# Where the attention's residual is turned for the ffn: from PE transposes to GpSimd's reordering, reads between the ffn's bursts and 32x32 turns on DVE

## The chip, the cores and the metric

The kernel runs on one core of one Trainium2 chip. The time is the device time of one execution in microseconds (us). The kernel before took 1957.53, 1955.65 and 1949.80 us in three runs; the median, 1955.65, is the time that the change is measured against.

In the profile's lines PE is TensorE's matmul unit, PEld its weight loading, DVE VectorE, ACT ScalarE, POOL GpSimd, SP SyncE (which here only issues DMAs); a q behind an engine's name is its queue of DMA issues. L1211 is line 1211 of the kernel before.

## What is computed

Two images of 128 channels and 64 x 64 positions pass two layers; everything is float32. Layer 0 (group norm, neighbourhood attention over 7 x 7 positions, layer norms and linear maps) isn't touched by the change. Layer 1 treats the 4096 positions as tokens `t` of 128 channels:

```python
t = _to_tokens(x)                       # [2, 4096, 128]
t = t + _L1_attn_ref(_ln_t(t))          # full self-attention, diagonal masked
t = t + _L1_ffn_ref(_ln_t(t), ...)
return _from_tokens(t, x)               # [2, 128, 64, 64]

def _stu(u, sigma, phi, Mu, Mpp, Mpm):  # what the ffn computes, for each of 4 lengths
    return _compute_spectral(u, sigma, phi, Mpp, Mpm) + _compute_ar_u(Mu, u)

def _compute_ar_u(Mu, u):               # three lags, each with a 128 x 128 matrix
    for i in range(Mu.shape[0]):
        ui = jnp.pad(u, ((0, 0), (i, 0), (0, 0)))[:, :sl]
        out = out + jnp.einsum('btd,de->bte', ui, Mu[i])
```

`_compute_spectral` convolves u causally with 16 filters along the tokens, once with and once without alternating signs, and applies a 128 x 128 matrix for each filter. The four lengths (all tokens, a half, a quarter, an eighth) are weighed by a hard choice (gumbel softmax). The change concerns the second line, `t + attention`, which has to be there twice: normalised as the ffn's input, and as it is, as the residual that the ffn's output is added to.

## The kernel before

**Stages.** Layer 0 takes the first 346 us. Then come the attention of image 0 (to about 720 us), that of image 1 (to about 1137), a tail that finishes image 1's last tokens (to 1199.6), the ffn of both images (to about 1920) and the last outputs.

**The attention** works on chunks of 512 tokens, eight to an image. Exponentials are made once for a pair of chunks (tiles `e`, 128 x 2048), sent through DRAM (`eb`) in 32-row pieces and turned by DVE, 32 x 32 at a time, into `et`, for the pair's other half. The chunk's result, channels by tokens, gathers in `xa[b]`. Work that isn't attention is handed out in small steps: after each step of the attention `fill()` takes the next step of the generators that wait, the urgent ones first.

**after(b, c)** is such a generator, one for each chunk that is complete. Four PE transposes bring xa's chunk to tokens by channels; DVE divides by the softmax's sum and adds it onto `tt[b]`, tokens by channels, so that `kept_` is the chunk of `t + attention`. Then come its layer norm (with a power on GpSimd), the transpose of the normalised tokens into `zc[b]`, channels by tokens, and the ffn's first transform: products with `tr` into two PSUM banks, which `store` copies into `uo` (ACT), adds and subtracts into `ub` (GpSimd; in the tail one of the two on DVE) and sends to `us` in DRAM. A chunk has four such stores of 128 rows (256 KB each), and its last 32 rows go out as eight small ones. During attention `fresh` queues these stores on GpSimd's queue, where `fill` issues them; in the tail (`crowd_[0] is None`) SP issues them at once. `ub` has four buffers and `uo` two.

**short_lags(b, h)** runs once for each half of an image. It first brings the residual into channels by tokens: four times, four PE transposes of `tt[b]` into a bank and a copy by ACT into `xa[b]` (L1209 to L1211). Then it makes four products of three lags each (L1221) out of `zc[b]`, and four DVE operations (six, where a length's boundary cuts the chunk) scale each by the branch's weight and add it onto xa (L1237). `residual_of` takes the first four steps in attention and the products are kept for later (`kept`, `held`); image 1's second half has its lags in the tail and the first bursts of the ffn.

**The tail** (L1547 on): the remaining chunks' generators take turns, and image 1's first lags are handed out between them; then the second half's transposes and two of its products.

**The ffn** has 160 blocks, 80 of each image. `burst` makes one block's 16 matmuls (K = 32 rows each, four at a time), four copies from PSUM into `y` (DVE, ACT, DVE, ACT) and starts the loads of a block four ahead: `ct` in four DMAs and `ut` in one, all on SP. `ct` has five buffers, `ut` four. Four bursts make one `y` (a group). `project` multiplies y by the filters' matrices, 16 k's for each of two signs, in the banks acc0 to acc3; a burst of the next group stands before every eighth k. `mixed_bins` empties the banks with four copies into `af` (DVE, ACT, DVE, ACT) and makes ten additions on GpSimd. `back` does the inverse transform of an image's first sixteen groups and adds it onto xa; `finished` does that of its last four and sends the output. Everything that is added onto xa must be there before `finished(b)` reads it. Only PE's order is written out by hand (`manual_schedule`); that of the other engines is made by the scheduler. The tiles of the ffn lie in the memory that the tail's tiles leave.

Of the kernel before, what the change touches and what calls it, by code (L numbers as in the profile page):

```python
# [14 lines left out]
P = 128  # L15
# [87 lines left out]
def kernel(  # L103
# [771 lines left out]
    gs = dram.tile([Q, 2, 2, SG, GROW], F32, name="gs")  # L875

    with ap_:
# [211 lines left out]
        queued_, turns_, crowd_ = [], [0, 0], [[]]  # L1089
# [28 lines left out]
        def after(b, c):  # L1118
# [19 lines left out]
            nc.vector.tensor_tensor(kept_[:, :, P - 1], kept_[:, :, P - 1], rest, ALU.subtract)  # L1138
            yield
# [14 lines left out]
            def store(pu, n, r0, m, ri):  # L1154

                for s in range(2):
                    both = sp.tile([P, 512], F32, tag="uo", name="uo", bufs=2)
                    nc.scalar.copy(both[:, 0 : 2 * n], pu[s][:, 0 : 2 * n])  # L1158
                    room()
                    ub = sp.tile([P, 2, 256], F32, tag="ub", name="ub", bufs=4)  # L1160
                    for sgn, op in enumerate((ALU.add, ALU.subtract)):
                        adder[sgn].tensor_tensor(ub[:, sgn, 0:n], both[:, 0:n], both[:, n : 2 * n], op)  # L1162
                    to = us[b, par, r0 : r0 + m, :, :, 2 * hh + s, 2 * fp : 2 * fp + 2]
                    if ri is not None:
                        fresh(to[:, :, ri].rearrange("k g f d -> k g (f d)"), ub)
                        continue
                    for sgn in range(2):
                        for f in range(2):
                            fresh(to[:, sgn, :, f].rearrange("k i d -> i k d"), ub[64 * f : 64 * f + 64, sgn, 0:P])
# [33 lines left out]
        def short_lags(b, h):  # L1203


            for par in range(2):
                n0 = (par * 2 + h) * 8
                for f0 in range(0, 8, 4):
                    pt = bank()  # L1209
                    transposed(pt, tt[b][:, n0 + f0 : n0 + f0 + 4, :])  # L1210
                    nc.scalar.copy(xa[b][:, (n0 + f0) * P : (n0 + f0 + 4) * P], pt)  # L1211
                    yield
            for par in range(2):
                for part_ in range(2):
# [16 lines left out]
                    for lo, hi in cut:  # L1231
                        t0 = c0 + lo * BLK
                        s = 0 if t0 < 256 else 1 if t0 < 512 else 2 if t0 < 1024 else 3
                        for e in range(2):
                            for i in range(NFP):
                                xs = xv[:, e, i, :, p0 + lo : p0 + hi]
                                nc.vector.scalar_tensor_tensor(  # L1237
                                    xs, pv[:, e, i, :, lo:hi], seg[:, s : s + 1], xs, ALU.mult, ALU.add
                                )
# [162 lines left out]
        def residual_of(lags):  # L1402
            for _ in range(4):
                next(lags)
                yield

        def filler(b, steps, kept, slow=()):
# [5 lines left out]
            def fill(c=None):  # L1413
                if c is not None:
                    done.append(c)
                    urgent.append(after(b, c))
                    if len(done) % 4 == 0:
                        lags = short_lags(b, len(done) // 4 - 1)
                        if kept is not None:
                            kept.append(lags)  # L1420
                            lags = residual_of(lags)
                        urgent.append(lags)
# [125 lines left out]
        *chains, residuals = left  # L1548
# [8 lines left out]
        for _ in residuals:  # L1557
            next(kept[0], None)
            next(held, None)
# [3 lines left out]
        for _ in range(2):  # L1563
            next(lags)
# [7 lines left out]
    with ExitStack() as cv:  # L1572
# [158 lines left out]

        order_ = [(b, q) for b in range(NB) for q in range(K2)]
# [3 lines left out]
        with tc.manual_schedule(engines={mybir.EngineType.PE}):  # L1736
            y = new_y()
            for i in range(4):
                if i % 2 == 0:
                    next(lags, None)  # L1740
# [10 lines left out]
            for i, (b, g) in enumerate(groups):  # L1751
# [3 lines left out]
                for l in range(2):  # L1755
                    for k in range(KF):
                        if following is not None and k % 8 == 0:
                            burst(following, 2 * l + k // 8)
                        project(y, acc, l, k)
# [138 lines left out]
```

## Time and profile before

| | us |
|---|---|
| median of the three runs | 1955.65 |
| the profiled execution | 1954.66 |
| its span, from first to last instruction | 1952.80 |

The span in stages, from the busy times of the engines in windows (us):

| stage | from, to | length | PE | DVE | ACT | POOL | DMA share |
|---|---|---|---|---|---|---|---|
| layer 0 | 0, 346 | 346.0 | 315.3 | 283.2 | 261.9 | 221.5 | 0.25 |
| attention, image 0 | 346, 720 | 374.0 | 370.4 | 189.0 | 116.9 | 152.7 | 0.67 |
| attention, image 1 | 720, 1137 | 417.0 | 412.6 | 189.2 | 126.6 | 180.0 | 0.68 |
| tail | 1137, 1199.6 | 62.6 | 55.7 | 37.1 | 18.1 | 17.8 | 0.25 |
| ffn | 1199.6, 1920 | 720.4 | 715.7 | 250.4 | 202.1 | 161.5 | 0.25 |
| last outputs | 1920, 1952.8 | 32.8 | 21.4 | 7.1 | 5.7 | 4.2 | 0.16 |

A row reads: in the ffn's 720.4 us PE was busy 715.7. The DMA share is that of the core's 16 DMA engines. Four groups of instructions by line, on which the change bears:

```profile
L1211 ACT COPY xa<-bank 128x512 f32<-128x512 f32 x16 | 9.1, 592 | 15.8 <-PE bank L202 15.8
L974 DVE STREAM_TRANSPOSE et<-et 128x512 f32<-128x512 f32 x216 | 134.2, 678 | 70.9 <-DMA et<-eb 70.8
L598 POOL COPY rb<-rden 128x512 f32<-128x512 f32 x16 | 9.8, 611 | 4.5 <-DVE rden L593 4.5
L1237 DVE SCALAR_TENSOR_TENSOR xa<-bank,seg,xa 128x128 f32<-128x128 f32 (+1 forms) x72 | 17.9, 312 | 7.0 <-PE bank L1221 7.0
```

The columns are: the line, the engine and operation, the tile written and those read, their shapes, and how many; then the busy time of all in us and the mean of one in ns; then the engine's idle time just before them, and what ended most of it. The first row: ACT copied 16 banks of 128 x 512 into xa, 592 ns each, and was idle 15.8 us in all before them, waiting for PE's transposes into the bank.

### The profile page before, as it was taken

To read this page: it belongs to the slowest core of one execution; us is meant where nothing else is said; L and a number is where in the kernel's file an instruction comes from. 1 tells how busy PE (TensorE), PEld (TensorE's weight loads), DVE (VectorE), ACT (ScalarE), POOL (GpSimd) and SP (SyncE) were. 2 spreads that over 40 slices of the span, in tenths; PEclk is the share of its full clock that TensorE was granted. 3 is DMA by queue.
4 is the path that set the end of the run, shared out by engine and by line. 5 is a ranking of instruction groups with operands and counts; after the bars stand their busy time and mean duration, and the time that the engine had idled before them with its cause. 6 is when DMAs were issued, how large, how long until landed. Compare 5 with 4: busy or idle time off the path is not lost.

```text
span 1952.8 us, 50772 instructions
## 1 busy us (share of the span) xinstructions
PE 1891.0 (97%) x20440; PEld 1347.5 (69%) x20440; DVE 956.0 (49%) x3026; ACT 731.3 (37%) x1718; POOL 737.7 (38%) x1209
## 2 busy tenths in 40 slices
PE   6899998999999999999999998999999999999997
PEld 3677776444444444444444456999999999999996
DVE  5799997454554534353454373333333333333332
ACT  2789887322233333232333222222222222222221
POOL 4366886424643335532425431122221121222211
PEclk9999999999999999999999999999999999999999
DMA  5222221667776544988867413222222223222211
GB/s 155 63 61 59 62 62 39 153 184 211 228 203 188 156 123 125 261 206 228 247 196 197 127 53 83 67 65 69 66 67 54 59 72 90 66 68 67 67 40 44
DMA packets 249769, 226.14 MB, mean 116 GB/s; under 512 B 126815, under 2 KB 204655, under 8 KB 242112
## 3 DMA queue, kind: packets, MB, share of 16 engines
q1 hardware_dynamic: 222786, 129.15, 27.5%
q10 hardware_dynamic: 8126, 58.04, 7.6%
q0 software_dynamic: 18624, 35.72, 6.3%
q8 instruction: 162, 2.65, 0.6%
q14 instruction: 71, 0.58, 0.1%
HBM read 131.40 MB, written 91.25 MB: 114 GB/s over the span
## 4 chain that ended last, share of the span: by engine, by line
PE 84%; DVE 5%; POOL 4%; DMA 2%; issue 1%; ACT 1%; SPq 0%; ACTq 0%; DVEq 0%; POOLq 0%
PE acc L1620 29%; PE own L984 12%; PE other L1057 9%; PE bank L926 9%; PE pc L1601 7%; PE bank L349 2%; PE bank L935 2%; PE bank L559 2%; PE bank L202 2%; PE bank L1177 1%; PE bank L1221 1%; PE bank L523 1%; ACT p L546 1%; PE po L581 1%; PE pc L1658 1%
## 5 line engine op out<-in xcount | busy, mean ns | idle before, releaser
L1606 DVE COPY y<-pc 128x512 f32<-128x512 f32 x320 | 206.2, 686 | 348.6 <-PE pc L1601 348.3
L1606 ACT COPY y<-pc 128x512 f32<-128x512 f32 x320 | 171.8, 589 | 402.5 <-PE pc L1601 396.9
L1620 PE MATMUL acc<-y,mpl 32*128 32x256 f32 x5120 | 321.6, 379 | 0.8 <-DVE af L1630 0.8
L1620 PE MATMUL acc<-y,mmi 32*128 32x256 f32 x5120 | 313.1, 375 | 0.0
L1620 PEld LDWEIGHTS acc<-y,mpl 32*128 32x128 f32 x5120 | 289.4, 186 | 7.3 <-DVE af L1630 1.7
L1620 PEld LDWEIGHTS acc<-y,mmi 32*128 32x128 f32 x5120 | 290.4, 185 | 2.6
L1631 POOL TENSOR_TENSOR af<-af 128x512 f32<-128x512 f32 x39 | 49.7, 1274 | 573.3 <-DVE af L1630 535.9
L1057 PE MATMUL other<-e,tok 128*128 128x512 f32 x448 | 227.5, 594 | 0.2
L931 ACT ACTIVATE e<-bank 128x512 f32<-128x512 f32 x216 | 129.1, 598 | 252.5 <-PE bank L926 241.8
L926 PE MATMUL bank<-cm 128*128 128x512 f32 x432 | 222.5, 601 | 0.0
L984 PE MATMUL own<-et,tok 128*128 128x512 f32 x448 | 212.1, 598 | 3.3 <-DVE et L974 3.2
L1601 PE MATMUL pc<-ct,ut 32*128 32x256 f32 x2560 | 208.3, 376 | 2.0 <-DVE y L1606 2.0
L1162 POOL TENSOR_TENSOR ub<-uo 128x256 f32<-128x256 f32 (+1 forms) x176 | 111.0, 666 | 176.4 <-ACT uo L1158 148.2
L1601 PEld LDWEIGHTS pc<-ct,ut 32*128 32x128 f32 x2560 | 170.1, 185 | 7.6 <-DVE y L1606 4.1
L974 DVE STREAM_TRANSPOSE et<-et 128x512 f32<-128x512 f32 x216 | 134.2, 678 | 70.9 <-DMA et<-eb 70.8
L984 PEld LDWEIGHTS own<-et,tok 128*128 128x128 f32 x448 | 85.7, 192 | 111.2 <-issue 96.1
L1057 PEld LDWEIGHTS other<-e,tok 128*128 128x128 f32 x448 | 81.5, 191 | 89.6 <-issue 82.1
L926 PEld LDWEIGHTS bank<-cm 128*128 128x128 f32 x432 | 76.3, 191 | 73.9 <-issue 67.7
L546 ACT ACTIVATE p<-p,mn 128x196 f32<-128x196 f32 x256 | 114.3, 449 | 14.4 <-DVE mn L536 13.9
L1093 POOL DMA_DIRECT2D us<-ub x158 | 108.0, 725 | 12.5 <-DMA us<-ub 10.1
L1158 ACT COPY uo<-bank 128x512 f32<-128x512 f32 (+1 forms) x96 | 45.4, 517 | 96.9 <-PE bank L1177 55.2
L1630 DVE COPY af<-acc 128x256 f32<-128x256 f32 x80 | 30.3, 420 | 104.6 <-PE acc L1620 104.6
(269 smaller groups left out, 2625.3 us busy)
## 6 DMA issues: line engine op xcount, KB each, us to landing
eb<-e ACTq DMA_DIRECT2D x54, 1024.0 KB
et<-eb SPq DMA_DIRECT2D x216, 256.0 KB
ut<-us SPq DMA_DIRECT2D x156, 128.0 KB
us<-ub POOLq DMA_DIRECT2D x54, 256.0 KB, 5.2
vw<-vd SPq DMA_DIRECT2D x256, 49.0 KB
ct<-gs SPq DMA_DIRECT2D x312, 40.0 KB
ct<-gs SPq DMA_DIRECT2D x312, 32.0 KB
vd<-v SPq DMA_DIRECT2D x128, 32.0 KB
```

Source lines behind the costliest of these rows:

```text
L546: nc.scalar.activation(p, p, AF.Exp, bias=t[name + "mn"][:, h : h + 1], scale=-1.0, accum_out=t["den"][:, u, h : h + 1],)
L926: nc.tensor.matmul(ps.rearrange("p (q t j) -> p q t j", q=4, t=4), lhsT=cm[b][:, n * P : (n + 1) * P], rhs=keys.rearrange("p (t q j) -> p ...
L931: nc.scalar.activation(e, ps.rearrange("p (q t j) -> p q t j", q=4, t=4), AF.Exp, bias=0.0, scale=ASCALE)
L974: in_place(nc.vector.transpose(part, part))
L984: nc.tensor.matmul(out_, lhsT=tok[b][:, n, :], rhs=e, start=first, stop=last, skip_group_check=True)
L1057: nc.tensor.matmul(turn(other, "p (q t j) -> p q t j"), lhsT=tok[b][:, n, :], rhs=es[j], start=(j == 0), stop=(j == 3),)
L1093: by.dma_start(out=to, in_=part)
L1162: adder[sgn].tensor_tensor(ub[:, sgn, 0:n], both[:, 0:n], both[:, n : 2 * n], op)
L1601: nc.tensor.matmul(pcs[j].rearrange("p (g o c) -> p o g c", g=4, o=2)[:, :, at], lhsT=ut[rows_, par, :], rhs=cv_[rows_], start=True, stop= ...
L1606: (nc.scalar.copy if j % 2 else nc.vector.tensor_copy)(y[:, :, :, 4 * kl + j, :], pcs[j].rearrange("p (g x k) -> p k g x", g=4, k=KF))
L1620: nc.tensor.matmul(acc[j][:, 0:256], lhsT=(mmi if l else mpl)[rows_, k, :], rhs=y[rows_, k, 2 * l : 2 * l + 2].rearrange("p s n x -> p (s ...
L1631: eng.tensor_tensor(af[:, 0:2], af[:, 0:2], af[:, 2:4], ALU.add)
```

## The change

1. `after`: when `kept_` is done, GpSimd copies it, with its channels' quarters in order, into the chunk's place in `xa[b]` (free by then), and a store of 256 KB takes it to `rd`, a new DRAM tile of 4.2 MB, by the queue that the other stores take.
2. `short_lags` loses the four groups of PE transposes with their copies; its products are written to xa, not added: for one half of the positions by a DVE operation, for the other by an ACT activation with the weight as its scale. `residual_of` goes, and the four products of image 1's second half stand before the ffn's first four bursts, one each.
3. `store` in the tail: copies and sums go into tiles of 128 x 2048 under the tags `e` and `et` in turn (two buffers of each) instead of `uo` and `ub`.
4. `residuals`, a new generator: for each of the 16 chunks four reads of 64 KB from `rd` into `rt` (one buffer), one quarter of the partitions each, with a step after each read; then a 32 x 32 transpose of rt on DVE in place, GpSimd's addition onto xa, and a step. One step is taken behind each of the ffn loop's bursts, for the first 80 of them.
5. SP's order in the ffn is written out by hand as PE's is.

```diff
@@ layer 1, tiles in DRAM @@
+    rd = dram.tile([NB, NT // 4, P, 4, P], F32, name="rd")
@@ after @@
             nc.vector.tensor_tensor(kept_[:, :, P - 1], kept_[:, :, P - 1], rest, ALU.subtract)
+            rq = xa[b][:, n0 * P : (n0 + 4) * P].rearrange("p (q j i) -> p q j i", q=4, j=4)
+            nc.gpsimd.tensor_copy(rq.rearrange("p q j i -> p j q i"), kept_.rearrange("p j (q i) -> p j q i", q=4))
+            fresh(rd[b, c].rearrange("p q r -> p (q r)"), xa[b][:, n0 * P : (n0 + 4) * P])
             yield
@@ store, in after @@
+                if crowd_[0] is None:
+                    free_[0] = not free_[0]
+                    if free_[0]:
+                        wide_ = ep.tile([P, 2048], F32, tag="e", name="wide").rearrange("p (a c) -> p a c", c=512)
+                    else:
+                        wide_ = ep.tile([P, 4, 512], F32, tag="et", name="wide", bufs=2)
                 for s in range(2):
-                    both = sp.tile([P, 512], F32, tag="uo", name="uo", bufs=2)
+                    if crowd_[0] is None:
+                        both, ub = wide_[:, s], wide_[:, 2 + s].rearrange("p (i c) -> p i c", i=2)
+                    else:
+                        both = sp.tile([P, 512], F32, tag="uo", name="uo", bufs=2)
                     nc.scalar.copy(both[:, 0 : 2 * n], pu[s][:, 0 : 2 * n])
-                    room()
-                    ub = sp.tile([P, 2, 256], F32, tag="ub", name="ub", bufs=4)
+                    if crowd_[0] is not None:
+                        room()
+                        ub = sp.tile([P, 2, 256], F32, tag="ub", name="ub", bufs=4)
@@ short_lags @@
-            for par in range(2):
-                n0 = (par * 2 + h) * 8
-                for f0 in range(0, 8, 4):
-                    pt = bank()
-                    transposed(pt, tt[b][:, n0 + f0 : n0 + f0 + 4, :])
-                    nc.scalar.copy(xa[b][:, (n0 + f0) * P : (n0 + f0 + 4) * P], pt)
-                    yield
...
-                                nc.vector.scalar_tensor_tensor(
-                                    xs, pv[:, e, i, :, lo:hi], seg[:, s : s + 1], xs, ALU.mult, ALU.add
-                                )
+                                if i:
+                                    nc.scalar.activation(
+                                        xs, pv[:, e, i, :, lo:hi], AF.Identity, bias=0.0, scale=seg[:, s : s + 1]
+                                    )
+                                else:
+                                    nc.vector.tensor_scalar(xs, pv[:, e, i, :, lo:hi], seg[:, s : s + 1], None, ALU.mult)
@@ filler and the tail @@
-                        lags = short_lags(b, len(done) // 4 - 1)
-                        if kept is not None:
-                            kept.append(lags)
-                            lags = residual_of(lags)
-                        urgent.append(lags)
+                        kept.append(short_lags(b, len(done) // 4 - 1))
...
-        *chains, residuals = left
+        chains = list(left)
...
-        for _ in residuals:
-            next(kept[0], None)
-            next(held, None)
...
-        for _ in range(2):
-            next(lags)
@@ the ffn @@
+        def residuals():
+            for b in range(NB):
+                for c in range(NT // 4):
+                    rt = cp.tile([P, 4, 4, 32], F32, tag="rt", name="rt", bufs=1)
+                    for q in range(4):
+                        nc.sync.dma_start(
+                            out=rt[32 * q : 32 * q + 32].rearrange("p h j i -> p h (j i)"),
+                            in_=rd[b, c].rearrange("(h p) q r -> q p h r", h=4)[q],
+                        )
+                        yield
+                    flat = rt.rearrange("p h j i -> p (h j i)")
+                    nc.vector.transpose(flat, flat)
+                    xs = xa[b][:, c * 512 : (c + 1) * 512].rearrange("p (j h r) -> p h j r", j=4, h=4)
+                    nc.gpsimd.tensor_tensor(xs, rt, xs, ALU.add)
+                    yield
+        to_add = residuals()
-        with tc.manual_schedule(engines={mybir.EngineType.PE}):
+        with tc.manual_schedule(engines={mybir.EngineType.PE, mybir.EngineType.SP}):
             y = new_y()
             for i in range(4):
-                if i % 2 == 0:
-                    next(lags, None)
+                next(lags, None)
                 burst(y, i)
...
                         if following is not None and k % 8 == 0:
                             burst(following, 2 * l + k // 8)
+                            next(to_add, None)
                         project(y, acc, l, k)
```

More of the change, by code (lines that the diff above doesn't have):

```diff
@@ L1088 @@
         adder = [nc.gpsimd, nc.gpsimd]
-        queued_, turns_, crowd_ = [], [0, 0], [[]]
+        queued_, turns_, crowd_, free_ = [], [0, 0], [[]], [False]
         def send_one():
@@ L1400, in filters @@
                     yield True
-        def residual_of(lags):
-            for _ in range(4):
-                next(lags)
-                yield
         def filler(b, steps, kept, slow=()):
@@ L1562 @@
         lags = kept[1]
-        for _ in range(2):
-            next(lags)
     outf = out.rearrange("b c h w -> b c (h w)")
```

## The prediction

> **What bounds the kernel now.** I read the engine totals, the slices and the chain of waits, then timelines and windows of the three stretches that the change touches. From the page:
>
> ```profile
> PE 1891.0 (97%) x20440; PEld 1347.5 (69%) x20440; DVE 956.0 (49%) x3026; ACT 731.3 (37%) x1718; POOL 737.7 (38%) x1209
> PE   6899998999999999999999998999999999999997
> PE 84%; DVE 5%; POOL 4%; DMA 2%; issue 1%; ACT 1%; SPq 0%; ACTq 0%; DVEq 0%; POOLq 0%
> L202 PE MATMUL bank<-ident,tt 128*128 128x128 f32 x64 | 9.8, 276 | 3.4 <-ACT uo L1158 3.4
> ```
>
> PE is busy 97% of the span and holds 84% of the chain, so PE work counts at its pitch, and other engines only where PE waits for them. The last row is the work that goes: 64 transposes of the attention's tokens, 16 groups of four. The timeline of the tail, from 1169 to 1200 us, behind the second attention (columns: start, duration, then the work, and in brackets the idle time before it and what ended it); PE's groups and the first y copy:
>
> ```profile
> 1170.63 0.66 PE L202 MATMUL bank<-ident,tt 128*128 128x128 f32 x4
> 1171.82 0.66 PE L202 MATMUL bank<-ident,tt 128*128 128x128 f32 x4 [0.53 <-ACT uo L1158]
> 1172.99 0.66 PE L202 MATMUL bank<-ident,tt 128*128 128x128 f32 x4 [0.52 <-ACT uo L1158]
> 1176.04 0.66 PE L202 MATMUL bank<-ident,tt 128*128 128x128 f32 x4 [2.40 <-ACT uo L1158]
> 1176.54 7.11 PE L1221 MATMUL bank<-tt,mu 128*128 128x512 f32 x12
> 1184.96 2.81 PE L1221 MATMUL acc<-tt,mu 128*128 128x512 f32 x6 [1.31 <-DVE xa L1237]
> 1188.92 1.29 DVE L1606 COPY y<-pc 128x512 f32<-128x512 f32 x2
> 1191.33 2.84 PE L1221 MATMUL acc<-tt,mu 128*128 128x512 f32 x6
> 1199.62 0.71 PE L1620 MATMUL acc<-y,mpl 32*128 32x256 f32 x8
> ```
>
> The tail isn't bound by PE: it idles between groups, and the y copy, whose burst ended before, starts only at 1188.92. y lies over the tail's buffers, so it waits for the last store out of them; by the queue events those land 0.8 us apart from 1182.25 to 1187.99. In the ffn (1199.6 to 1920) PE is packed, 715.65 of 720.40 us. One burst there and its followers:
>
> ```profile
> 1403.44 0.38 PE L1601 MATMUL pc<-ct,ut 32*128 32x256 f32 x2
> 1403.52 1.29 DVE L1606 COPY y<-pc 128x512 f32<-128x512 f32 x2 [3.03 <-PE pc L1601]
> 1403.89 0.36 SPq L1497 DMA_DIRECT2D ut<-us  x1
> 1404.30 2.45 SPq L1489 DMA_DIRECT2D ct<-gs  x4
> 1407.14 0.76 DVE L1630 COPY af<-acc 128x256 f32<-128x256 f32 x2 [2.33 <-PE acc L1620]
> 1407.89 1.29 DVE L1606 COPY y<-pc 128x512 f32<-128x512 f32 x2
> 1408.04 1.27 POOL L1631 TENSOR_TENSOR af<-af 128x512 f32<-128x512 f32 x1 [12.94 <-DVE af L1630]
> ```
>
> The burst ends near e = 1403.44; af copies at e+3.7 empty the banks that the next group's products need, and the next y copies follow at e+4.4.
>
> **Parts and costs.** The basis is the profiled execution, 1954.66 us (span 1952.80 plus 1.86 around it); the median of the three runs is 1955.65, 0.99 above, so each sum carries over with +0.99. I call 0.5%, 9.8 us, what a measurement of this kernel tells from no change.
>
> 1. PE transposes out. Eight PE transposes stand as 0.87 us in the chain at 1119.30 (L980), 0.109 each: a group of four is 0.435, and 16 groups 6.96. Twelve groups lie in the attentions, where PE is busy 445 of 450 us: -5.2. The last four lie in the tail, costed in 4. If those steps had merely filled other gaps, it is 0; so 0 to -7.0. ACT loses 16 copies of 592 ns, mostly off the path.
>
> 2. Reordering and storing, in attention. 16 GpSimd copies of 128x512; the trace has no reordering one, so the bounds are 611 ns (L598) and 1274 (L1631, with two inputs), 1 us taken. Fourteen stores at 725 ns to issue on GpSimd's queue (L1093); the last two go on SP's. Together some 14 x (1 + 0.725) = 24 us of GpSimd, 3% of the 800 us of attention, in which it is busy 43% (192 of 450). Behind a copy in order wait its sums (L1162) and stores and the layer norm's power of its own chunk; that waits anyway for DVE's statistics, some 1.7 us, which is the cover. Without it the copies and stores cost up to 24. The cost is taken at 0. The extra 4.2 MB share the queues with the bounced exponentials, which have one visible collision:
>
> ```profile
> 910.80 2.49 DVE L974 STREAM_TRANSPOSE et<-et 128x512 f32<-128x512 f32 x4 [4.16 <-DMA et<-eb]
> 911.57 2.93 PE L984 MATMUL own<-et,tok 128*128 128x512 f32 x3 [3.17 <-DVE et L974]
> 880.00:920.00 40.00, 36.83 (x87) 16.63 (x86) 16.49 (x31) 9.82 (x23) 13.31 (x20) 0.91 0.89 242
> ```
>
> PE lost 3.2 us there, and its granted clock was half for 6.83 us, some 3.4 more: 6.6. Shifted transfers may move such a stall, remove it, or make new ones: -6.6 to +13, taken at 0.
>
> 3. Lags written by two engines. Each product shows as six 128x512 matmuls, 2.84 us at 1191.33 with the last one's end, so about 2.6 in a row. Before, four DVE operations took 1.13; now DVE and ACT alternate on one tile's rows, each possibly waiting for the other: 2 x 0.31 (L1237) + 2 x 0.45 (L423) plus hand-overs, 1.9. It's under the product's 2.6 and hidden but for the last of a run: 0 to +3 for some eight runs, +1 taken.
>
> 4. Tail. The sums go into wider buffers, so the waits for an ub buffer (DVE 2.85 at 1174.58, GpSimd 2.29 at 1174.61) go, and the last chunk's second store of 128 rows, issued 1178.79 and landed 1181.2, comes about when its neighbours do, 1180.3. Eight small stores at 0.8 apart follow: 1180.3 + 8 x 0.8 = 1186.7 instead of 1187.99, and the first y copy just behind, 1186.9 instead of 1188.92: -2. The two stores of rd (256 KB) and one lag product more stand ahead of the first project (two lie behind the first y copy, since each stands before its own burst, formerly one): +2.6. PE, done with its transposes sooner, idles some 8 us before, and a drop of the clock costs about 1.7 (the two products at 1176.54 took 7.11 where 2 x 2.6 = 5.2 is full pace, under one half-clock record of 3.41 us), of which 1.2 on the path. Sum +1.8. If the stores drain at SP's issue pace (last issue 1183.9), -4.9; if rd's stores delay them by 4 us, +5.
>
> 5. The ffn. 64 reads, 16 transposes on DVE, 16 adds on GpSimd. SP's order is now written: ut (waits for the burst), the read, four ct. Per burst SP issues 0.36 + 0.40 (taken between its neighbours) + 2.45 = 3.2 of 4.3 us where it had 2.8: a read holds the four ct behind it up by 0.4, and no more. Blocks are loaded four bursts (17 us) ahead. A read is issued at e+0.86 and lands, at ut's median of 2.16 (of 149), at e+3.0; the 0.68 transpose (L974) is over at e+3.7. Though written behind the next burst, it stands on DVE right behind the y copies of the very burst whose end releases the last read of its chunk: DVE's order is the scheduler's, SP's the written one. In 12 of 16 chunks the next work on DVE is at e+4.4: nothing. In four (0, 4, 8, 12) the af copies are due at e+3.7: 0 to 0.3 each, 1.1 at the 90th percentile of landings (3.26); one such delay makes the next group's first products late. So 0 to +3, +1 taken. The adds, 1.27 (L1631), end near e+5, or, in the four chunks whose add comes with mixed bins (which fill GpSimd from 1408.04 to 1412.5), up to e+9.5; the next chunk's first read goes into rt two bursts on, at e+9.5. Without that cover an add is 16 x 1.27 = 20.
>
> Sum: -5.2 + 0 + 1 + 1.8 + 1 = **-1.4**; 1955.65 - 1.4 = **1954.2**, and by the bounds of its terms (-7 to 0, 0 to 3, -4.9 to 5, 0 to 3) mostly 1946 to 1962.
>
> The Trainium skill speaks to the size of a stall in 5: "TensorE: Matmul & The Clock Gate", section "Why this matters for your kernels", has the clock drop for idle gaps over about 3 us. The trace has a drop to half for 3.41 us after 1.40 us of idling at 1853.06 and none after 2.51 at 1564.58. So the row doesn't bear the threshold out: a stall under 3 us may be charged with 1.7 more, by the page with nothing; in rival A that is 18 against 11.
>
> **Rivals.**
>
> A, slower: the reads come late and DVE, in order, holds the af copies. If SP's read lands like the ct behind it, at e+5.5 or later, the four places cost (5.5 + 0.7 - 3.7 = 2.5, with its semaphore 2.8) x 4 = 11.2, and each stall, if it catches the clock as at 1853, 4 x 1.7 = 6.8: 18 in place of +1, 1971. It decides from landings later than e+3.0. Against: ut's p90 of 3.26 would only make e+4.1. For: 512 B rows, four gathers, and DMA share is 25% already. 0.15.
>
> B, slower: the added 4.2 MB and the shifted filter loads make two more collisions as at 908, at 6.6 each: +13.2, 1967. For: DMA share 0.89 there. Against: one in 800 us so far, and 4.2 MB are under 3% of the stretch's traffic (183 GB/s x 800 us = 146 MB). 0.15.
>
> C, faster: the tail drains at SP's pace (-4.9 for +1.8) and the stall at 908 vanishes (-6.6): 1954.2 - 6.7 - 6.6 = 1940.9. 0.25.
>
> That the transposes go out of attention but the time doesn't, since the steps filled gaps, is 0 instead of -5.2: 1959.4, inside my own range; it has 0.1 of the 0.45 for no change.
>
> **How the numbers follow.** Forecast 0.45 (with the case just named), A and B 0.30, C 0.25: faster by over 9.8 us 0.25, within 0.45, slower 0.30. The time is the likeliest's, 1954. The range reaches to C's 1941 and past B's 1967 toward A's 1971: 1941 to 1970.
>
> **What would show it.** Right: no L202 row out of tt; no waits on ub in the tail; the first y copy near 1186.7 less the 5 us gained before it; ffn length within 3 us of 720.4; rt's transpose waiting for a DMA, and PE waiting under 0.5 us after mixed bins. Wrong: PE idle behind a DVE transpose of rt (A), more waits at L974 for et<-eb (B), a tail shorter by 5 us (C). The forecast would fall if the stores of rd, on GpSimd's queue, delayed the exponentials' chain for many chunks, which the trace can't show.

## The result

Over 21 runs each the changed kernel took 1957.26 us in the median (1951.12 to 1963.02), the kernel before 1952.21 (1948.31 to 1957.53): 1.0023 times, with a 95% interval of 1.0014 to 1.0032. By the ratio that is 4.5 us slower (2.7 to 6.2; the two medians lie 5.0 apart), inside the stated range and inside the 9.8 us of "no change", but on the other side of the forecast's -1.4. The three runs shown beforehand had a median 3.4 us above that of the 21.

The profiled execution took 1956.34 us, its span 1954.4. The engine totals and PE's slices on its page, which answer to those shown of before (line numbers in what follows are those of the kernel that was profiled):

```profile
PE 1885.4 (96%) x20376; PEld 1343.4 (69%) x20376; DVE 960.3 (49%) x3002; ACT 734.7 (38%) x1742; POOL 775.9 (40%) x1255
PE   6899998999999999999999998999999999999997
```

PE has the 64 transposes less (20440 - 20376) and 5.6 us less work, GpSimd 38 us more; the span is 1.6 us longer all the same. I cut both profiles at events that both have: the first and last of the 216 exponentials that DVE turns later (ACT at L931 in before, at L932 in after; the attention goes on for some 40 us behind the last of them), the first y copy, the first y copy of the second group (where project starts), the end:

| stretch, us | before | after | difference |
|---|---|---|---|
| to the first exponential (layer 0, untouched) | 352.4 | 353.8 | +1.3 |
| to the last exponential | 739.8 | 733.2 | -6.6 |
| to the first y copy | 96.7 | 94.7 | -2.0 |
| to the first y copy of the second group | 10.6 | 15.1 | +4.5 |
| to the end | 753.3 | 757.7 | +4.4 |

So the attention and the stores' end gained what was expected, the last lags and the ffn gave it back. But these are one execution each, and the second row's gain may not be typical: two other kernels whose attention is the same as after's (lags_first and turn_phase, below) took 738.9 and 736.9 us there, 0.9 and 2.9 less than before.

**Attention.** The timeline around 777 us, first of before, then of after (DVE's turn of the bounced exponentials and PE's products with them):

```profile
776.43 2.49 DVE L974 STREAM_TRANSPOSE et<-et 128x512 f32<-128x512 f32 x4 [7.68 <-DMA et<-eb]
777.68 1.88 PE L984 MATMUL own<-et,tok 128*128 128x512 f32 x4
```

```profile
762.78 0.62 POOL L1141 COPY xa<-tt 128x512 f32<-128x512 f32 x1
767.91 0.59 POOL L1094 DMA_DIRECT2D rd<-xa  x1
768.51 1.52 POOL L1309 DMA_DIRECT2D st<-in_m_plus_dram  x2
779.52 2.49 DVE L975 STREAM_TRANSPOSE et<-et 128x512 f32<-128x512 f32 x4 [11.18 <-DMA et<-eb]
780.33 1.96 PE L985 MATMUL own<-et,tok 128*128 128x512 f32 x4 [2.90 <-DVE et L975]
```

DVE's wait for the bounced exponentials is 11.18 us instead of 7.68, and PE waits 2.90 us for DVE where it hadn't waited at all. Around it the filter loads `st` are new: eight are issued on GpSimd's queue from 762.0 to 798.8, where before had three, the first at 792.91. The windows of the two, 760 to 800 us (length, then the busy times of PE, PEld, DVE, ACT and POOL, the clock, the DMA share, GB/s), of before and of after:

```profile
760.00:800.00 40.00, 40.00 (x125) 18.17 (x124) 18.79 (x57) 13.77 (x24) 24.76 (x37) 1.00 0.88 249
```

```profile
760.00:800.00 40.00, 37.10 (x117) 16.61 (x116) 17.52 (x52) 12.51 (x23) 28.30 (x42) 1.00 0.93 282
```

The loads moved because `filler` begins with them once fewer than four generators wait, and the residual's generator, left over from image 0, is no longer one of them. The granted clock is full in both.

**The last lags.** After's timeline of PE (its groups only):

```profile
1182.32 2.88 PE L1597 MATMUL pc<-ct,ut 32*128 32x256 f32 x16 [5.94 <-ACT y L1602]
1185.13 4.40 PE L1228 MATMUL acc<-tt,mu 128*128 128x512 f32 x6
1190.53 2.84 PE L1228 MATMUL acc<-tt,mu 128*128 128x512 f32 x6
1196.87 3.47 PE L1616 MATMUL acc<-y,mpl 32*128 32x256 f32 x57
```

PE idles 5.94 us for the first y copy, the clock falls to half (6.83 us from 1181.5), so that the burst takes 2.88 and the next lag product 4.40 instead of 2.84; a second product follows. The first project starts at 1196.87, 15.2 us after the first y copy at 1181.68; before it was 10.7.

**The ffn.** One of the four places where a chunk's transpose stands directly ahead of the af copies, in after's timeline:

```profile
1297.69 0.47 SPq L1734 DMA_DIRECT2D rt<-rd  x1
1300.55 0.65 ACT L1626 COPY af<-acc 128x256 f32<-128x256 f32 x2 [2.51 <-PE acc L1616]
1301.29 0.71 DVE L1740 STREAM_TRANSPOSE rt<-rt 128x512 f32<-128x512 f32 x1 [3.08 <-DMA rt<-rd]
1301.92 0.72 DVE L1626 COPY af<-acc 128x256 f32<-128x256 f32 x2
1302.37 2.00 PE L1616 MATMUL acc<-y,mpl 32*128 32x256 f32 x28 [0.83 <-DVE af L1626]
```

ACT's af copies run at 1300.55, DVE's wait behind the transpose, which waits for the read, until 1301.92, and PE waits for them. By ACT's y copies the group's pace is 17.27 to 17.35 us, and groups with such a transpose took 17.68, 18.70 and 17.87. The fourth is the last ahead of the inverse transform:

```profile
1476.06 0.72 DVE L1626 COPY af<-acc 128x256 f32<-128x256 f32 x2
1476.22 1.27 POOL L1742 TENSOR_TENSOR xa<-rt,xa 128x512 f32<-128x512 f32 x1 [12.71 <-DMA ct<-gs]
1477.44 1.27 POOL L1627 TENSOR_TENSOR af<-af 128x512 f32<-128x512 f32 x1
1480.78 1.60 PE L1667 MATMUL pc<-ident,ob 128*128 128x128 f32 x4 [1.52 <-POOL ob L1640]
```

and in before, where by chance the same transposes start at the same time:

```profile
1480.78 1.98 PE L1671 MATMUL pc<-ident,ob 128*128 128x128 f32 x8 [1.00 <-POOL ob L1644]
```

In after af is late, GpSimd's add stands ahead of mixed bins besides, and PE's transposes wait 1.52 us where they waited 1.00 before; then the clock is half for 3.41 us from 1481.84, which it wasn't before. That group took 26.46 us instead of 24.02. Only a part of this is the change's: of the six kernels that have this add ahead of mixed bins all wait 1.52 or 1.53 us, but three have no fall there (after_crowd3, below: 25.04 us for the group), and before_no_turn, whose ffn is before's, has one from 1480.14 behind a wait of 1.01 us.

### The profile page after: what moved, and what is told of

Its sections match the earlier page's. It is cut to its first block, busy times and chain, and to the rows that moved or that the text cites. A ratio compares the mean times of both kernels' runs of the same rounds, so it can differ in the third digit from the quotient of the medians.

```text
span 1954.4 us, 50851 instructions
## 1 busy us (share of the span) xinstructions
PE 1885.4 (96%) x20376; PEld 1343.4 (69%) x20376; DVE 960.3 (49%) x3002; ACT 734.7 (38%) x1742; POOL 775.9 (40%) x1255
## 5 line engine op out<-in xcount | busy, mean ns | idle before, releaser
L932 ACT ACTIVATE e<-bank 128x512 f32<-128x512 f32 x216 | 129.0, 598 | 257.8 <-PE bank L927 253.6
L1176 POOL TENSOR_TENSOR ub<-uo 128x256 f32<-128x256 f32 (+1 forms) x160 | 99.8, 662 | 148.9 <-ACT uo L1171 136.0
L943 ACT ACTIVATE e<-bank 128x512 f32<-128x512 f32 (+1 forms) x72 | 32.5, 455 | 124.6 <-DVE bank L941 113.3
L536 DVE CUSTOM_DVE_ANT_0 p<-bank,tab 128x196 f32<-128x196 f32 x256 | 76.4, 353 | 4.9 <-PE bank L523 4.7
```

The lines of the kernel that those rows point to most:

```text
L536: nc.vector.tensor_tensor_reduce(t[name + "p"][:, h, :], t[name + "S"][h][:, 0:KEYS], tab[:, ci, h, :], 1.0, 3.0e38, ALU.add, ALU.min, t[n ...
L932: nc.scalar.activation(e, ps.rearrange("p (q t j) -> p q t j", q=4, t=4), AF.Exp, bias=0.0, scale=ASCALE)
```

## The experiments

Each ran beside the kernel before on the same chip, so the ratios to it are compared. Three undo one suspected loss each, the fourth all three.

**lags_first**

```diff
+            for _ in lags:
+                pass
             for i in range(4):
-                next(lags, None)
                 burst(y, i)
-            for _ in lags:
-                pass
```

> The changed kernel with all four lag products of image 1's second half ahead of the first burst, instead of one before each of the first four bursts. Theory (order in the tail): in the changed kernel PE idles 5.94 us before its second burst (1176.38 to 1182.32), waiting for the first y copy, and the products behind that copy, 4.40 and 2.84 us long, then hold up the bursts; put ahead, two of them fill the idle time, the distance from the first y copy to the first project falls from 15.2 to about 8.3 us (four bursts at the 2.1 us of y's copies), PE's clock does not fall at 1181, and the time falls by 6 to 7 us. Rival (the tail ends with its stores and loads whatever PE does): the first project comes at the same distance, and the time moves by under 1.5 us.

Measured: 1.0016 (1.0007 to 1.0024), against after's 1.0023: 1.4 us, not 6 to 7, and the intervals overlap. In its profile the distance from first y copy to project did fall, from 15.2 to 8.8 us:

```profile
1184.60 1.15 PE L1597 MATMUL pc<-ct,ut 32*128 32x256 f32 x16
1187.67 1.73 PE L1597 MATMUL pc<-ct,ut 32*128 32x256 f32 x16 [1.92 <-DVE y L1602]
1189.78 1.73 PE L1597 MATMUL pc<-ct,ut 32*128 32x256 f32 x16 [0.38 <-DVE y L1602]
```

PE's wait for the first y copy is 1.92, the bursts follow at 2.1 us. So the place of the lags is shown to make the 4.5 us there. What it gained was lost again elsewhere in this execution: the attention, which the edit doesn't touch, took 738.9 us instead of 733.2, and the ffn took 759.5 instead of 757.7, since PE waited 1.99 us for the first af copies behind a transpose (under 0.25 in after). SP is what was late there:

```profile
1209.81 1.29 DVE L1602 COPY y<-pc 128x512 f32<-128x512 f32 x2 [3.03 <-PE pc L1597]
1213.24 0.47 SPq L1734 DMA_DIRECT2D rt<-rd  x1
1215.40 0.71 DVE L1740 STREAM_TRANSPOSE rt<-rt 128x512 f32<-128x512 f32 x1 [4.30 <-DMA rt<-rd]
```

The last read was issued 3.4 us behind the start of its burst's y copies (0.8 in after's chunk at 1297): the first bursts now come every 2.1 us, and a burst's five loads hold SP for over 3, in written order. The clock fell too, at 1194 instead of 1181. That the late read cost what the lags gained isn't shown: the ffn's 1.8 us in one execution don't make up the 4 that are missing between 5.7 us in the tail and 1.4 in the ratio.

**turn_phase**

```diff
+            for _ in range(2):
+                yield
             for b in range(NB):
...
-                        yield
+                        if q < 3:
+                            yield
```

> The changed kernel with a chunk's residual in four steps (the last read, the transpose and the add share one), started two bursts later, so that the transpose of every chunk stands behind the second burst of a group and the add never just before mixed bins. Theory (the four transposes that stand ahead of the af copies cost the ffn its 4.2 us: 0.41, 1.35, 0.52 and 0.50 us late af copies, and the last of them makes the inverse transform late by 0.5 and the clock fall for 3.41 us): groups of the ffn's first image all take 17.27 to 17.35 us, the distance from first project to the end falls from 757.6 to about 753.4, and the time falls by 4 us. Rival (the reads share the DMA queues with ut and ct, and it is these that come late): the lost time stays, spread otherwise, and the time moves by under 1 us.

Measured: 1.0006 (0.9993 to 1.0019), 3.3 us under after. The ffn took 753.6 us, before's 753.3. Its timeline at such a transpose:

```profile
1292.82 0.71 DVE L1743 STREAM_TRANSPOSE rt<-rt 128x512 f32<-128x512 f32 x1 [2.40 <-DMA rt<-rd]
1293.46 1.28 DVE L1602 COPY y<-pc 128x512 f32<-128x512 f32 x2
1301.29 0.76 DVE L1626 COPY af<-acc 128x256 f32<-128x256 f32 x2 [2.23 <-PE acc L1616]
```

The transpose still waits for its read, but only y copies come behind it, and the af copies wait only for PE. The other runs agree: counted from the second group's y copy, the ffn takes 756.0 to 759.5 us in the six kernels with the transposes where the change put them, 752.5 to 755.0 in the four with them moved, 753.5 in one without the residual's path and 753.3 to 755.1 in the three that have before's ffn. The theory stands; the reads themselves cost nothing that these runs can tell.

**filters_held**

```diff
-                if len(steps) < 4 and turns_[0] % 2:
+                if len(steps) < 3 and turns_[0] % 2:
```

> The changed kernel with the ffn's filter loads held until one generator less is waiting, so that they start where they started before the change (in the changed kernel they start some 20 us earlier, at 761, because the residual's steps no longer stand in the list). Theory (the moved filter loads collide with the bounced exponentials: the waits of 2.90, 0.70 and 0.91 us at 777, 847 and 901): these waits shrink to under 2 us in all, and the time falls by about 3 us. Rival (the 256 KB stores of the residual make them, wherever the filters are): waits of this kind stay at 4 to 5 us, and the time moves by under 1 us.

Measured: 1.0000 (0.9990 to 1.0010), 4.5 us under after, and the two intervals don't meet. The loads start at 793.0, 31 us later than in after (not some 20, as was expected). The window of 760 to 800 us has PE busy throughout again, at a DMA share of 0.83:

```profile
760.00:800.00 40.00, 40.00 (x125) 18.28 (x124) 15.98 (x41) 12.58 (x22) 24.14 (x36) 1.00 0.83 244
```

The waits at 777 and 847 are gone; one of 4.3 us at 903, with 6.83 us at half clock, stands in this execution where before has its own at 908 and after two of 0.9 and 0.5. The two other kernels with the early loads, lags_first and turn_phase, waited 5.02 and 5.09 us for the same exponentials, each with a half clock of 3.41 us behind it; turn_phase's row:

```profile
780.02 3.37 PE L985 MATMUL own<-et,tok 128*128 128x512 f32 x4 [5.09 <-DVE et L975]
```

So by the runs' times the loads' early start costs about 4.5 us, and it makes this stall; the three kernels that have the loads early have 5 or 6 of them issued between 12 us before these reads of the bounced exponentials and their use, and PE waits 2.90 to 5.09 us, while in the eleven others none is issued then and PE waits at most 1.16. Whether the stall is where the 4.5 us go is another question, for the table of the attention further down.

**three**: the three edits together.

> The three edits together: lags ahead of the bursts, transposes behind a group's second burst, filter loads where they were. If all three theories hold the sum is -6.5 - 4 - 3 = -13.5 from the changed kernel, about 1943.7, 8.5 under the kernel before; if only the tail's holds, about 1951, level with the kernel before; if the first two hold, 1947.

Measured: 1948.94 us against 1952.95, 0.9979 (0.9969 to 0.9989). From after's 1.0023 that is 8.6 us; the single edits had 1.4, 3.3 and 4.5, in sum 9.2. Two thirds of the expected gain: of the three single edits it was the lags' that fell short, with 1.4 of 6.5.

The second four: what the parts are worth.

**before_no_turn**

```diff
-                    pt = bank()
-                    transposed(pt, tt[b][:, n0 + f0 : n0 + f0 + 4, :])
-                    nc.scalar.copy(xa[b][:, (n0 + f0) * P : (n0 + f0 + 4) * P], pt)
                     yield
```

> The kernel before without the 64 PE transposes of the residual and their 16 copies, everything else in its place (the steps stay, empty; the products are added onto what attention left in xa, so the residual is left out of the output). Theory (PE is packed in attention, so the twelve groups there are worth their 5.2 us, and the four in the tail nothing): the time is 5.2 us under the kernel before, 0.9973 of it. Rival (the steps filled gaps): within 1.5 us of it, over 0.999.

Measured: 0.9981 (0.9966 to 0.9995), -3.7 us, between the two. The table below shows where the rest is: without its waits the attention is shorter by some 5 to 6 us, but PE's waits for the bounced exponentials are longer.

**no_rd_held**: filters_held, and

```diff
-            nc.gpsimd.tensor_copy(rq.rearrange("p q j i -> p j q i"), kept_.rearrange("p j (q i) -> p j q i", q=4))
-            fresh(rd[b, c].rearrange("p q r -> p (q r)"), xa[b][:, n0 * P : (n0 + 4) * P])
...
-        to_add = residuals()
+        to_add = iter(())
```

> The changed kernel with the filter loads held, and without the residual's new path: no reordering copies, no stores and reads of rd, no transposes and adds (the residual is left out of the output). It is compared with filters_held, which stood at 1.0000 of the kernel before. Theory (the path costs only what its transposes do in the ffn): 4.2 us under filters_held, 0.9978 of the kernel before, with the ffn's groups all at 17.27 to 17.35 us and the wait near 905 us in attention still there. Rival (the stores of rd and the copies cost in attention or in the tail too): 7 us or more under it, 0.9964 or less, with the wait near 905 gone or the first y copy sooner after the attention.

Measured: 0.9988 (0.9975 to 1.0002), 2.3 us under filters_held, where the theory had 4.2 and the rival 7 or more. The ffn took 753.5 us, the tail 95.1 (94.9 in filters_held), and the wait near 905 is there without a single store of rd:

```profile
909.58 3.78 PE L985 MATMUL own<-et,tok 128*128 128x512 f32 x4 [5.92 <-DVE et L975]
```

So the stores of rd and the copies on GpSimd cost nothing that these runs can tell.

**old_tail_held**: filters_held, with `if False:` and `if True:` for the two tests of `crowd_[0]` in `store`, so that the tail uses uo and ub.

> The changed kernel with the filter loads held, and with the tail's copies and sums in the old buffers uo and ub. It is compared with filters_held (1.0000 of the kernel before). Theory (the wide buffers bring the last chunk's stores and so the first y copy some 2 us forward): from the last exponential to the first y copy 2 us longer, the time 2 us longer, ratio 1.0010. Rival (the small stores' 0.8 us apart set the end, whatever the buffers): the distance within 0.5 us, the time within 1 us. A third: the wide buffers cost more than they bring, since y lies over them, and the time is shorter without.

Measured: 1.0013 (1.0001 to 1.0025), 2.5 us over filters_held. From the last exponential to the first y copy it took 96.4 us, filters_held 94.9. DVE and GpSimd wait for a buffer again, as in before:

```profile
1175.46 1.15 DVE L1176 TENSOR_TENSOR ub<-uo 128x256 f32<-128x256 f32 x2 [2.76 <-DMA us<-ub]
1175.50 2.01 POOL L1176 TENSOR_TENSOR ub<-uo 128x256 f32<-128x256 f32 x3 [2.22 <-DMA us<-ub]
```

So the wide buffers bring the first y copy 1.5 us forward, near the 2 forecast. But the first project starts no sooner for it, 109.2 us behind the last exponential in filters_held and 109.1 here, since 14.3 us lie between y copy and project there and 12.7 here; and the intervals of the two ratios overlap. That the wide buffers shorten the whole is not shown.

**dve_lags_held**: filters_held, and

```diff
-                                if i:
+                                if False:
                                     nc.scalar.activation(
```

> The changed kernel with the filter loads held, and with all four operations of a lag product on DVE instead of two on DVE and two on ACT in turn. It is compared with filters_held (1.0000 of the kernel before). Theory (the turns between the engines, 0.4 us of waiting at each, lie behind PE's next product): the time within 1 us. Rival (the chain of four is on the path in the tail, where it stands ahead of the y copies: 1.6 us now, 1.2 on one engine, four times): 1 to 2 us shorter.

Measured: 1.0005 (0.9994 to 1.0017) against 1.0000, no difference that can be told. The turns between DVE and ACT cost nothing that this run shows.

The attention stretches tell why part of the PE gain doesn't arrive. From each profile: the length from first to last exponential, as above; PE's waits over 0.4 us before the products with the bounced exponentials (two others of 0.45 us and one of 0.57, which every kernel has, left out); the time at half clock, of which half is taken as lost (four of these products take 3.78 us at half clock, 1.88 in the row at 777.68); and what is left:

| kernel | length | waits | half clock | rest |
|---|---|---|---|---|
| before | 739.8 | 3.2 | 6.83 | 733.2 |
| before_no_turn | 739.0 | 8.3 | 6.83 | 727.3 |
| after | 733.2 | 5.0 | 0 | 728.2 |
| lags_first | 738.9 | 8.4 | 6.83 | 727.2 |
| turn_phase | 736.9 | 7.6 | 3.41 | 727.6 |
| filters_held | 735.1 | 4.3 | 6.83 | 727.4 |
| no_rd_held | 737.7 | 6.6 | 6.83 | 727.8 |
| three | 736.0 | 4.5 | 6.83 | 728.2 |

The rest falls by 5.0 to 6.0 us in these kernels without the transposes, near the 5.2 that were worked out (it is good to about 1 us, since the half clock begins inside the wait in most rows and is then partly counted twice). But all wait somewhere from 900 to 915, where the bounced exponentials' reads pass at a DMA share of 0.94 and more (from the first read's issue to the data's use), and most of those without the transposes wait longer there than before's 3.2 us: 5.3 in before_no_turn, 5.9 in no_rd_held. Counted from the first exponential, PE is ready for these products at 555.6 us in before_no_turn and 552 to 554 in the held kernels, where before was at 556.0; the data are used at 556.4 to 560.9, in before at 559.1.

The table also limits what can be said of the moved loads. The three kernels with early loads took 733.2 to 738.9 us in this stretch, filters_held and the four others that hold them in the same way 734.8 to 737.7: what the held kernels save at 777 they wait longer near 905 (4.1 to 5.9 us, the three 1.4 to 3.3). So the runs show that the loads' early start costs 4.5 us (the intervals of after and filters_held don't meet), but these profiles, one execution each, don't show it in the length of the attention, and where it goes as a whole stays open. The wait near 905 was the next bound, so two kernels went after it.

**three_slow3** and **three_crowd3**: the three edits, and

```diff
-                if len(steps) < 3 and turns_[0] % 2:
+                if len(steps) < 3 and turns_[0] % 3 == 0:
```

in the first, in the second

```diff
-                if len(steps) < 3 and turns_[0] % 2:
+                if len(steps) < 3 and turns_[0] % 2 and len(queued_) < 3:
```

> The kernel with the three edits, and with the ffn's filter loads taken at every third turn instead of every second, so that they are spread wider over image 1's attention. Theory (the wait of 4.45 us near 905 with its 6.83 us at half clock is the bounce queueing behind filter loads and the eight small stores of a chunk, since the DMA share there is 0.9 and up): the wait falls under 2 us, no half clock follows, the attention takes 730 instead of 736 us, and the time falls by 4 to 7 us, ratio 0.995 to 0.996. Rival (the small stores and the bounce collide there without filters): the wait stays at 4 us or more, the time within 1.5 us of the three edits' (0.9979). If the spread loads run past the attention, the tail grows instead.

> The kernel with the three edits, and with filter loads taken (at every second turn, as there) only while fewer than three stores wait in the list, so that they keep out of the way of the small stores. Theory as for three_slow3: the wait near 905 shrinks, ratio 0.995 to 0.996. Rival: it stays, 0.9979. Where this one helps and three_slow3 doesn't, it is the loads' place beside the small stores and not their rate.

Measured: 1943.32 us, 0.9952 (0.9936 to 0.9969), and 1942.45 us, 0.9952 (0.9934 to 0.9970), against 1953.24 of the kernel before: 9.4 us faster, and the best of the study. The windows of 880 to 920 us, three and then three_crowd3:

```profile
880.00:920.00 40.00, 35.55 (x85) 16.02 (x84) 17.23 (x32) 9.45 (x21) 12.95 (x19) 0.91 0.78 206
```

```profile
880.00:920.00 40.00, 40.00 (x105) 18.66 (x104) 17.67 (x34) 10.70 (x24) 9.07 (x13) 1.00 0.81 222
```

PE is busy in all of the 40 us, its clock full, and the core moves more (222 GB/s for 206). (three_crowd3's profile is of the fastest of its six runs, 1936.07 us.) Over the whole kernel the products with bounced exponentials wait 0.8 us instead of 4.8; the attention takes 727.8 and 729.5 us. It isn't the stores alone: from 12 us before the reads that PE waited for until their data were used, three issued six filter loads and eight stores, three_slow3 three and eight, three_crowd3 three and nine, and the data were used 14.2, 10.6 and 10.2 us behind the first read's issue. With as many stores and fewer filter loads among them the wait is gone. Both forms do it; rate and place can't be told apart.

**before_crowd3** and **after_crowd3**: the same rule alone, in before (with its `< 4`) and in after.

> The kernel before, with filter loads taken only while fewer than three stores wait in the list; nothing of the change. Theory (the wait near 908 belongs to the kernel before as much as to the changed one): the wait of 3.17 us and its half clock vanish, attention takes 733 instead of 740 us, ratio 0.9966 to 0.998. Rival (it is the residual's stores that the rule helps): over 0.999.

> The changed kernel with the same rule for the filter loads (and held as in filters_held), but with its lags and transposes where the change put them. Theory (the change by itself, without its collisions in attention, is -5.2 for the transposes, -2 to the first y copy, +4.5 to the first project, +4.2 in the ffn, sum +1.5): 1 to 2 us over before_crowd3, and 4 to 6 us over three_crowd3 by the two edits it lacks, ratio near 0.998. Rival (the change gains once the collisions are gone): 4 us or more under before_crowd3.

Measured: 0.9988 (0.9976 to 0.9999) and 0.9992 (0.9982 to 1.0002) of the same 1952.77. In before the rule helped less than expected: a wait of 2.2 us at 906 and 3.41 us of half clock stayed, and its attention took 738.2. after_crowd3 had none (729.8), yet is level with before_crowd3, because it takes 14.3 us from first y copy to project and 756.7 in the ffn. three_crowd3, without these two losses, stands 7.8 us under it. That is more than the 4 to 6 expected, and the theory's 1 to 2 us over before_crowd3 came out as 0.8. The change as it was made is a draw with the attention cleared; with its steps placed it is some 7 us ahead (0.9952 against 0.9988, intervals that don't meet, though measured on two chips). One of these steps, the lags ahead of the bursts, could be tried in before as well, where 10.7 us pass from the first y copy to the project and 8.8 in three_crowd3; that wasn't run, so up to 2 of the 7 us may not be the change's.

## Why the prediction was wrong

The forecast was -1.4 us; +4.5 was measured (2.7 to 6.2). Two terms failed.

Step 2 failed, as it was put: "Shifted transfers may move such a stall, remove it, or make new ones: -6.6 to +13, taken at 0." They made one, at 777, and undoing the shift alone took 4.5 us off the time. (The stall is the moved loads'; that the 4.5 us are its price is not shown, as the table of the attention says.) The step's bounds held it, though the list of bounds under the sum, which gave 1946 to 1962, left this step's out. Rival B named the shifted filter loads, but wanted two more collisions and gave them 0.15. The 0 was chosen as a middle, when the moved loads could have been followed to what they meet from 762 us on: the DMA share of before was 0.88 there already. The rest of that step was right as far as no_rd_held can tell: GpSimd's copies and the 4.2 MB of rd cost nothing in the attention or the tail.

Step 5 named the right place, the four transposes ahead of the af copies, and mis-sized it: 0 to 0.3 us each and +1 in all, where the af copies were late by 0.41, 1.35, 0.52 and 0.50. With a fall of the clock behind the fourth that makes 4.4 us in after's profile; by the ratio of turn_phase it is 3.3. The fall was partly bad luck: it comes in three of the six kernels with that add. The read was reckoned to be issued at e+0.86 and to land at e+3.0, e being the end of its burst. At three of the four places it was issued at e+1.2 to e+1.4, behind ut, and the transpose started at e+3.4 to e+3.6; at the other it was issued at e+0.85, but the transpose started only 3.13 us after the issue's end, as in one more of the sixteen chunks (1.69 to 1.95 us in the others). Rival A's mechanism, then, at a quarter of its price.

Step 1 was right about PE: the rest of the attention fell by 5.0 to 6.0 us, 5.2 forecast. But it took the whole of it as gained; before_no_turn gained 3.7 of it (1.0 to 6.6), for the waits for the bounced exponentials lengthen, the one near 905 most. Step 3 took +1 for the lags on two engines; nothing of it shows in dve_lags_held. Step 4 was nearly right: -2.0 to the first y copy as forecast, and +4.5 behind it where 2.6 + 1.2 were forecast. The clock did fall there.

Put together, -3.7 for the transposes, 4.5 for the shifted loads, 2.5 for the tail and 3.3 for the ffn make 6.6, not 4.5. Each of these is good to one or two us at best, so the account doesn't close better than that.

Case C's other half, the vanishing of the wait at 908, didn't come by itself in most kernels. It is worth nearly what C put on it, though: three_crowd3, in which it is gone, stands a further 5.3 us below three (0.9952 against 0.9979, intervals that just touch).

The prediction's reading of the clock took the idle time of the weight loads, 1.40 and 2.51 us; the matmuls' own waits at the two places are 1.00 and 2.11. Its conclusion holds with either.

## What to carry to other kernels

When an edit takes a step out of a list by which other steps are paced, follow those others: here removing a generator made filter loads start 31 us earlier, into a stretch with a DMA share of 0.88, and that cost about as much as the PE work that was saved. In this ffn a transpose on DVE that waits for a DMA costs nothing that shows where y copies follow it, and 0.4 to 1.4 us where the copies follow that free PE's banks; so choose its period so that it never meets that place. And where a stretch is almost bound by a transfer, a PE saving ahead of it is partly paid back in the wait (1.5 of 5.2 us in before_no_turn): look for the next bound before booking the gain.

## What the runs showed of the hardware

The granted clock's fall isn't told by the length of the wait before it. In after PE waited 2.90 us at 777 and the clock stayed full; 5.09 us at 775 in turn_phase was followed by 3.41 us at half. One wait of 1.52 us, at 1479 in after, was followed by 3.41 us at half, and one of the same length before the same transposes, at 1472 in after_crowd3, by none. A wait of 2.1 us ahead of other transposes, at 1566 in after and at 1562 in turn_phase, was followed by no fall in the one and by 3.41 us in the other. Before itself has 3.41 us at half behind a wait of 1.00 us at 1853 and none behind one of 1.00 us at 1480. The Trainium skill ("TensorE: Matmul & The Clock Gate", section "Why this matters for your kernels") has the fall behind idle gaps over about 3 us; the wait of 1.52 us in after contradicts it as a bound.

A read of 64 KB in rows of 512 B was usable by DVE 1.69 to 1.95 us after its issue had ended in fourteen of sixteen chunks, and 3.13 us after in two, in one and the same stretch of after's ffn, whose mean DMA share is 0.27; in the other kernels the longest was 3.55 us (filters_held).
